# A sandwich of attention and feed-forward on one core: low halves on ScalarE's queue, products of block 1 ahead of the first scores, and a centred projection

## The chip, the cores and the metric

The kernel runs on one core of one Trainium2 chip. The metric is the device time of one execution in microseconds (us). The engines are named as the profile names them: PE (TensorE, matrix products), PEld (its weight loads), DVE (VectorE), ACT (ScalarE), POOL (GpSimd) and SP (SyncE, which only issues transfers here). ACT and POOL can issue transfers too; a transfer issue stands in the engine's own instruction order, so whatever the issue waits for, the instructions behind it wait for as well.

## What is computed

x is 4096 x 256, float32. With `ln` for a layer norm without weights:

```
x = x + ln(attention(ln(x)))          # 16 heads of 16, causal, out @ w_proj + b_proj
x = x + ln(ffn(ln(x)))                # 256 -> 1024 (gated) -> 1024 -> 1024 -> 256, ternary weights with scales
```

The part that the change touches is the inner `ln` behind the attention's projection: for each token, y = out @ w_proj + b_proj, then (y - mean(y)) / sqrt(var(y) + 1e-5), where mean and variance run over the 256 outputs of that token.

## The kernel before, in words

**Blocks.** The 4096 tokens are cut into eight blocks j = 0..7 of 512 (`QB`), each block into four tiles of 128 (`NT`). The 16 heads are cut into four groups g = 0..3. The attention walks through 32 items (j, g) in order. An item has 4j + 3 steps (`steps`, L876); a step makes one or two units of scores, 128 keys for 512 queries in two heads side by side, so a unit is 128 x 1024. The item (j, g) has 8j + 5 units, and the whole attention has 1056.

**A unit** goes through three engines. PE makes the scores into one of three PSUM buffers (`ps_s`, L843), DVE takes their maximum (L852), ACT takes their exponential into a tile `e` (L859). The maxima are not used by the same block's exponentials: they give the shift of the next block (`next_shift`, L1026) and a check at the end. Only block 0 takes its shift from its own first two units (L1171). On the diagonal POOL then clears what lies above it (L866). Later PE multiplies `e` with the values (L930) into one PSUM bank, which ACT copies out when the item is done (L953), and SP stores it.

**Queries and keys** are needed as a high half and a low half of each number (hi, lo). `features` (L519) makes them for half of the heads: two products into a bank (L525, `pk` or `pq`), an ACT pass that adds the bias (L534, tile `full`), a rounding to `hi` (L542) and the difference `lo` (L544). For blocks 0 and 1 DVE makes both halves, for the others POOL. Each half is then stored to DRAM twice (L549), in transfers of 8 heads x 16 x 512, and loaded again as rows of a head pair (L557). The tiles `full`, `hi` and `lo` exist once for keys and once for queries, so a second set waits for the stores of the first. The queue of a store is chosen at L548: for blocks 0 and 1 the low halves go by POOL's queue, all others by SP's.

**Background work.** `prep(j)` (L599) loads a block, normalises it, transposes it (L633), makes keys and queries for both halves of the heads, then the values (L650). `project(j)` (L273) gathers the finished attention of block j, multiplies by the weights `wp` (L314), adds the bias `bp`, makes the layer norm and stores `x1[j]`. Both are generators: every `yield` says what kind of piece comes next (PE, ACT or any). `Background.even` (L95), called after a step, gives at most one PE piece and one ACT piece for every 1 to 3 steps, depending on the block; `step` (L63) runs the next piece of the oldest job, and `finish` (L112) runs all that is left of a named job. `prep(j+2)` is added in item (j, 1), `project(j)` when the last item of block j has ended. In item (j, 3) the keys and queries of block j + 1 are forced if they are not there yet (L1137). `halve_weights` (L981) is a third job: four POOL passes (L1009 to L1012) on a piece of a feed-forward weight, one piece for every four steps.

**The layer norm in `project`** takes, for each of the four tiles of a block but the last one, one ACT pass for the mean (`mean_of`, L199, accumulating at L203), one ACT pass for the squared distances from it (`spread_of`, L207, at L211), then on POOL 1/sqrt (L215), shift and scale (L223) and the addition of x (L351). Each ACT pass is a piece of its own.

**The start** (L1102 to L1132) is written out by hand: the statistics of blocks 0 and 1, then `biases` (L1102), which folds the values' bias through `wp` into `bp` by one product (`pb`, L1106), then `prep(0)` up to the queries of the first half of the heads, the loads for the first two items, the rest of `prep(0)`, and then the walk over the items. `prep(1)` has only been normalised by then; its products run as pieces during block 0.

**Semaphores of transfers.** In the built program the transfers that SP and ACT issue take eight semaphores in turn, and one that takes a semaphore again first waits until the transfer that had it before has landed. POOL's transfers have eight others.

After the attention come the feed-forward layers, which start when the last block has ended; nothing in them is changed.

Of the kernel before, what the change touches and what calls it, by code (L numbers as in the profile page):

```python
# [10 lines left out]
F32 = mybir.dt.float32  # L11
F32R = mybir.dt.float32r
AF = mybir.ActivationFunctionType
ALU = mybir.AluOpType
AX = mybir.AxisListType
# [102 lines left out]
def sandwich_kernel(  # L118
# [80 lines left out]
    def mean_of(src, mv, t):  # L199

        lent.append(True)
        junk = const.tile([P, D], F32, tag="junk", name="junk")
        nc.scalar.activation(  # L203
            junk, src, AF.Identity, scale=-1.0 / D, accum_out=mv[:, t, 0:1]
        )

    def spread_of(src, mv, t):  # L207

        lent.append(True)
        junk = const.tile([P, D], F32, tag="junk", name="junk")  # L210
        nc.scalar.activation(  # L211
            junk, src, AF.Square, bias=mv[:, t, 0:1], accum_out=mv[:, t, 1:2]
        )

    def rstd_of(mv):  # L215
# [57 lines left out]
    def project(j, room):  # L273

        last = j == NB - 1
        xj = room.block(j)
        nc.sync.dma_start(out=xj, in_=rows(x, j))

        sums = stat.tile([P, H * QB // P], F32, tag="sums", name=f"sums_{j}")
        heads = weighed[j].rearrange("g (h e) n -> (g h) e n", e=HW)
        nc.sync.dma_start(out=sums, in_=heads[:, HD, :].rearrange("h (a n) -> h a n", a=8))
        for _ in range(5 if 1 < j < NB - 1 else 3):
            yield True
        if not last:
            nc.vector.tensor_reduce(least[:, j : j + 1], sums, AX.X, ALU.min)
        nc.vector.tensor_scalar(sums, sums, 1.0e-30, None, ALU.max)
        nc.vector.reciprocal(sums, sums)
        yield Background.HEAD  # L290
        nc.sync.dma_start(out=inverse[j].rearrange("h (a n) -> (h a) n", a=8), in_=sums)
        oT, inv = room.features(j)
        for c in range(DC):
            mine = slice(8 * c, 8 * (c + 1))
            nc.sync.dma_start(out=oT[:, c, :], in_=heads[mine, 0:HD, :])
            nc.sync.dma_start(
                out=inv[:, c, :],
                in_=inverse[j][mine, None, :].to_broadcast([8, HD, QB]),
            )
        for _ in range(4):  # L300
            yield True
        for c in range(DC):
            nc.gpsimd.tensor_tensor(oT[:, c, :], oT[:, c, :], inv[:, c, :], ALU.mult)
            yield True
        yield True
        yield Background.PE
        y = room.tokens(j)
        mv = stat.tile([P, NT, 2], F32, tag="mv", name=f"mvy_{j}")
        for half in range(0, NT, 2):
            ps = room.bank(f"py_{j}_{half}").rearrange("p (t f) -> p t f", t=2)  # L310
            for t in range(2):
                yield room.within(t)
                for c in range(DC):
                    nc.tensor.matmul(  # L314
                        ps[:, t, :],
                        lhsT=oT[:, c, (half + t) * P : (half + t + 1) * P],
                        rhs=wp[:, c, :],
                        start=(c == 0),
                        stop=(c == DC - 1),
                    )  # L320
            if last:
                nc.vector.tensor_tensor(
                    y[:, half : half + 2, :],
                    ps,
                    bp[:, None, :].to_broadcast([P, 2, D]),
                    ALU.add,
                )
                for t in range(half, half + 2):
                    layernorm_stats(y[:, t, :], mv, t)
            else:  # L330
                lent.append(True)
                nc.scalar.copy(y[:, half : half + 2, :], ps)
                nc.gpsimd.tensor_tensor(
                    y[:, half : half + 2, :],
                    y[:, half : half + 2, :],
                    bp[:, None, :].to_broadcast([P, 2, D]),
                    ALU.add,
                )
            yield Background.PE if half < NT - 2 else Background.ACT
        if not last:  # L340
            for t in range(NT):
                mean_of(y[:, t, :], mv, t)
                yield Background.ACT
                spread_of(y[:, t, :], mv, t)
                yield Background.ACT if t < NT - 1 else True
        rstd = (layernorm_rstd if last else rstd_of)(mv)
        for t in range(NT):
            (normalize if last else shift_and_scale)(
                y[:, t, :], y[:, t, :], mv, rstd, t, nc.gpsimd
            )  # L350
            nc.gpsimd.tensor_tensor(y[:, t, :], y[:, t, :], xj[:, t, :], ALU.add)  # L351
            yield True
        nc.sync.dma_start(out=rows(x1[j], 0), in_=y)
        yield True
# [49 lines left out]
    def attention(shared):  # L404
# [8 lines left out]
        with ExitStack() as actx:  # L413
# [19 lines left out]
            def two_banks(name):  # L433
                return ps_s.tile([P, 2, QB], F32, tag="s", name=name)
# [84 lines left out]
            def features(j, s, c, engine):  # L519
# [25 lines left out]
                for half, part in enumerate((hi, lo)):  # L545
                    for d in range(2):
                        at = (d, half) if i else (half, d)
                        queue = nc.gpsimd if shared and j < 2 and half else nc.sync  # L548
                        queue.dma_start(  # L549
                            out=halves_of[s, j][8 * c : 8 * (c + 1), at[0], at[1]], in_=part  # L550
                        )
# [549 lines left out]

            def biases():  # L1102
                nc.vector.tensor_scalar(bqk[:, 0:DC], bqk[:, 0:DC], SCALE, None, ALU.mult)
                ps = two_banks("pb")[:, 0, 0:D]
                for c in range(DC):
                    nc.tensor.matmul(  # L1106
                        ps,
                        lhsT=bv[:, c : c + 1].to_broadcast([P, P]),
                        rhs=wp[:, c, :],
                        start=(c == 0),  # L1110
                        stop=(c == DC - 1),
                    )
                nc.vector.tensor_tensor(bp, bp, ps, ALU.add)

            works = [prep(0, nc.vector), prep(1, nc.gpsimd)]
            for work in works:
# [10 lines left out]
            if shared:  # L1127
                bg.add(("prep", 1), works[1], PREP)
                bg.work[0][3] = Background.PE
            else:  # L1130
                while bg.piece(works[1]) is not False:
                    pass  # L1132
            mxs = {}
            for n, (j, g) in enumerate(items) if shared else ():
# [14 lines left out]
                if (j, g) == (NB - 1, G - 2):  # L1149
                    for _ in halving:  # L1150
                        pass
                    bg.add(("norm", 0), norm_block(0, room, first_features), NORM)
                if (j, g) == (NB - 1, G - 1):
                    W["h1"] = weight_pieces("h1", TAGS["h1"])
# [353 lines left out]
```

## Time and profile before

| what | value |
|---|---|
| median of 3 runs | 2053.86 us (2051.06 to 2056.44) |
| the profiled execution: its own time | 2048.42 us |
| span of the profiled execution, first to last instruction | 2046.5 us |
| first maximum of block 0 | 39.81 us |
| first maximum of block 1 | 92.84 us |
| last maximum of the attention ends | 1374.5 us |
| PE busy over the span | 1825.3 us (89%) |
| DVE busy over the span | 1609.8 us (79%) |
| ACT busy over the span | 1399.2 us (68%) |
| mean granted PE clock | 0.986 |

How to read what follows. A line of the timeline gives the start, the duration, the engine, the line in the kernel, the operation and its tiles; "x4" says that four such instructions are merged, and in brackets stands how long the engine sat idle before and who ended that. A line of the stage windows gives, for a stretch of the span, its length and then for each engine its busy time and its number of instructions, the granted clock of PE, the mean busy share of the 16 DMA engines and the bytes moved. "SPq" and "ACTq" are transfer issues, which don't count as busy time.

### The profile page before, as it was taken

Reading aid. Unit: us, or ns where it says so; the run is one execution under the profiler, and the core shown is the slowest. Engines: PE = TensorE matmul, PEld = TensorE weight load, DVE = VectorE, ACT = ScalarE, POOL = GpSimd, SP = SyncE. Lnnn points to the kernel's source line nnn. Section 1 sums busy time; section 2 is a strip of 40 time slices with the busy share of each in tenths; the row PEclk is TensorE's granted clock in tenths of the full one; section 3 lists DMA queues with packets and bytes.
Section 4 is the critical chain, followed back from the end, with each engine's and each line's share of the span. In section 5 each row is a group of like instructions: output and inputs, shape, how many; then the busy total and the mean of one; then the engine's idle time right before and its main releaser. Section 6 shows DMA issues by size and latency. Waiting matters only on the chain.

```text
span 2046.5 us, 28401 instructions
## 1 busy us (share of the span) xinstructions
PE 1825.3 (89%) x10518; PEld 932.5 (46%) x10518; DVE 1609.8 (79%) x1894; ACT 1399.2 (68%) x1598; POOL 552.2 (27%) x871
## 2 busy tenths in 40 slices
PE   4799989988888888888888887889999999999997
PEld 2333332322322322223222222228888888888886
DVE  3689998998999999999999999985546456465453
ACT  2699999999999999999999998982212222222221
POOL 3264545434435335333333110000120000000000
PEclk8899999999999999999999998999999999999999
DMA  6756645444235333553234213103100000000000
GB/s 168 229 179 219 191 133 180 147 154 159 98 131 183 116 103 124 161 163 115 76 136 156 98 44 101 63 9 114 53 11 21 15 7 21 1 21 21 1 11 15
DMA packets 134909, 202.09 MB, mean 99 GB/s; under 512 B 16064, under 2 KB 60736, under 8 KB 134752
## 3 DMA queue, kind: packets, MB, share of 16 engines
q1 hardware_dynamic: 130496, 194.56, 29.3%
q0 software_dynamic: 2480, 4.35, 1.0%
q8 instruction: 87, 1.43, 0.3%
q10 hardware_dynamic: 1776, 1.18, 0.3%
q14 instruction: 70, 0.57, 0.1%
HBM read 137.91 MB, written 62.13 MB: 98 GB/s over the span
## 4 chain that ended last, share of the span: by engine, by line
PE 46%; ACT 21%; DVE 19%; issue 6%; DMA 4%; POOL 2%; SPq 1%; ACTq 0%; POOLq 0%; DVEq 0%
PE z L1358 21%; ACT e_s L859 19%; DVE mx L852 18%; PE av L930 7%; PE s L843 7%; PE za L1358 3%; PE zb L1358 2%; PE pyf L1440 2%; DMA k<-k 1%; PE py L314 1%; PE pk L525 1%; PE pv L650 1%; PE pq L525 1%; ACT junk L211 1%; DMA q<-hiq 0%
## 5 line engine op out<-in xcount | busy, mean ns | idle before, releaser
L852 DVE TENSOR_REDUCE mx<-s 128x1 f32<-128x1024 f32 x1056 | 1219.8, 1217 | 72.1 <-PE s L843 66.6
L859 ACT ACTIVATE e_s<-s,shift 128x1024 f32<-128x1024 f32 x1056 | 1153.6, 1117 | 104.9 <-DVE mx L852 81.9
L843 PE MATMUL s<-q,k 64*128 64x512 f32 (+3 forms) x2304 | 517.7, 468 | 161.2 <-ACT e_s L859 144.7
L930 PE MATMUL av<-e_s,v 128*32 128x512 f32 (+2 forms) x4576 | 572.8, 575 | 7.9 <-POOL e_s L866 5.7
L843 PEld LDWEIGHTS s<-q,k 64*128 64x128 f32 x2304 | 208.9, 185 | 752.9 <-ACT e_s L859 652.2
L1425 ACT ACTIVATE fb<-z,sh 128x512 f32<-128x512 f32 x128 | 88.1, 689 | 364.8 <-PE z L1358 340.2
L1358 PE MATMUL z<-hb_0l,h 128*128 128x512 f32 x512 | 199.5, 390 | 0.0
L1358 PE MATMUL z<-hb_0h,h 128*128 128x512 f32 x512 | 199.5, 390 | 0.0
L866 POOL TENSOR_SCALAR_AFFINE_SELECT e_s<-e_s 128x256 f32<-128x256 f32 (+1 forms) x224 | 94.7, 440 | 337.4 <-ACT e_s L859 337.4
L233 POOL TENSOR_TENSOR rstd<-ve,neghalf 128x4 f32<-128x4 f32 (+1 forms) x22 | 20.8, 944 | 608.8 <-DVE ve L231 603.0
L930 PEld LDWEIGHTS av<-e_s,v 128*32 128x32 f32 x4576 | 97.2, 109 | 151.5 <-issue 116.1
L1325 DVE CAST hb_1h<-fb 128x512 fp32r<-128x512 f32 x64 | 27.4, 428 | 155.7 <-ACT fb L1425 155.7
L1402 ACT ACTIVATE sl<-za,s 128x512 f32<-128x512 f32 x64 | 44.0, 690 | 120.4 <-PE za L1358 60.9
L1325 DVE CAST hb_0h<-fb 128x512 fp32r<-128x512 f32 x64 | 28.1, 440 | 99.6 <-ACT fb L1425 99.6
L1358 PEld LDWEIGHTS z<-hb_0h,h 128*128 128x128 f32 x512 | 96.1, 188 | 20.0
L1358 PEld LDWEIGHTS z<-hb_0l,h 128*128 128x128 f32 x512 | 96.2, 188 | 19.8
L1011 POOL TENSOR_SCALAR wc<-wc 128x256 f32<-128x256 f32 x88 | 75.8, 861 | 7.8
L1010 POOL TENSOR_TENSOR wc<-wc,wh 128x256 f32<-128x256 f32 x88 | 64.3, 730 | 7.2
L1012 POOL TENSOR_TENSOR fit<-fit,wc 128x256 f32<-128x256 f32 x88 | 64.2, 730 | 7.3
L1009 POOL CAST wh<-wc 128x256 fp32r<-128x256 f32 x88 | 35.0, 397 | 108.4 <-DMA wc<-in_h_t_dram 75.9
L1440 PE MATMUL pyf<-w,hb_1l 128*128 128x256 f32 x256 | 61.8, 284 | 0.0
L1440 PE MATMUL pyf<-w,hb_1h 128*128 128x256 f32 x256 | 61.7, 283 | 0.0
(257 smaller groups left out, 1970.3 us busy)
## 6 DMA issues: line engine op xcount, KB each, us to landing
k<-k SPq DMA_DIRECT2D x288, 256.0 KB
q<-q SPq DMA_DIRECT2D x64, 256.0 KB
x<-in_x_dram SPq DMA_DIRECT2D x16, 512.0 KB
k<-hik SPq DMA_DIRECT2D x32, 256.0 KB
q<-hiq SPq DMA_DIRECT2D x32, 256.0 KB
wc<-in_h_t_dram SPq DMA_DIRECT2D x64, 128.0 KB
r_h<-wh SPq DMA_DIRECT2D x64, 128.0 KB
h<-r_h SPq DMA_DIRECT2D x32, 256.0 KB
```

Of the source, the lines that this page charges most:

```text
L843: nc.tensor.matmul(self.both[:, i, col : col + n], lhsT=kT[G * j + g, c, pr][r, tt * P : (tt + 1) * P], rhs=qT[j, g][pr][r, QB - n :], sta ...
L852: nc.vector.tensor_reduce(next(columns), self.both.rearrange("p a n -> p (a n)"), AX.X, ALU.max)
L859: nc.scalar.activation(e, self.both, AF.Exp, bias=shifts[j])
L866: nc.gpsimd.affine_select(out=here, in_=here, compare_op=ALU.is_ge, fill=0.0, base=0, pattern=[[0, here.shape[1]], [1, P]], channel_multip ...
L930: nc.tensor.matmul(self.av[h * HW : (h + 1) * HW, QB - n :], lhsT=vb[kt // NT][:, kt % NT, o : o + HW], rhs=of(es, h), start=(kt == 0 or k ...
L1010: nc.gpsimd.tensor_tensor(w, w, hi, ALU.subtract)
L1011: nc.gpsimd.tensor_scalar(w, w, 0.0, None, ALU.is_equal)
L1012: nc.gpsimd.tensor_tensor(fit, fit, w, ALU.mult)
L1325: nc.vector.tensor_copy(hi, full)
L1358: nc.tensor.matmul(ps, lhsT=w[c], rhs=single(part[:, c, :]), start=(c == 0 and i == 0), stop=(c == kc - 1 and i == parts - 1),)
L1425: nc.scalar.activation(h, z, AF.Gelu, scale=sc[:, oc : oc + 1])
L1440: nc.tensor.matmul(ps[:, 0:D], lhsT=single(part[:, c, t * P : (t + 1) * P]), rhs=(w3_r if halves else w3_sb)[:, c, :], start=(c == 0 and i ...
```

## The change

It has four parts.

1. The queue of the low halves (L548): for block 0 they are issued by ACT instead of POOL; block 1 stays on POOL, the others on SP.
2. Before the walk over the items, `prep(1)` is stepped until the keys of its first half of the heads are stored: two groups of four transposes and the two products of one `pk`, with the copies, rounding and stores that belong to them. These then stand ahead of the first scores in the order of PE, ACT and DVE.
3. In `biases` the projection weights are centred in place: each row of `wp` (one input, 256 outputs) loses its mean over the outputs, before the product `pb` reads it; after `pb` is added, `bp` loses its own mean. Then every y has mean zero, and for all blocks but the last, `project` leaves the mean pass out, takes the squares about 0.0 and scales without a shift.
4. Ahead of the item (7, 2), `project(6)` is finished by force before the norm of block 0 is added.

```diff
-    def spread_of(src, mv, t):
+    def spread_of(src, mv, t, shift=None):
...
-            junk, src, AF.Square, bias=mv[:, t, 0:1], accum_out=mv[:, t, 1:2]
+            junk,
+            src,
+            AF.Square,
+            bias=mv[:, t, 0:1] if shift is None else shift,
+            accum_out=mv[:, t, 1:2],
         )
...
             for t in range(NT):
-                mean_of(y[:, t, :], mv, t)
-                yield Background.ACT
-                spread_of(y[:, t, :], mv, t)
+                spread_of(y[:, t, :], mv, t, 0.0)
                 yield Background.ACT if t < NT - 1 else True
         rstd = (layernorm_rstd if last else rstd_of)(mv)
         for t in range(NT):
-            (normalize if last else shift_and_scale)(
-                y[:, t, :], y[:, t, :], mv, rstd, t, nc.gpsimd
-            )
+            if last:
+                normalize(y[:, t, :], y[:, t, :], mv, rstd, t, nc.gpsimd)
+            else:
+                nc.gpsimd.tensor_scalar(
+                    y[:, t, :], y[:, t, :], rstd[:, t : t + 1], None, ALU.mult
+                )
...
-                        queue = nc.gpsimd if shared and j < 2 and half else nc.sync
+                        queue = (nc.scalar, nc.gpsimd)[j] if shared and j < 2 and half else nc.sync
...
             def biases():
                 nc.vector.tensor_scalar(bqk[:, 0:DC], bqk[:, 0:DC], SCALE, None, ALU.mult)
+                mean = stat.tile([P, DC], F32, tag="mean", name="mean")
+                nc.vector.tensor_reduce(mean, wp, AX.X, ALU.add)
+                nc.vector.tensor_scalar(mean, mean, -1.0 / D, None, ALU.mult)
+                for c in range(DC):
+                    nc.vector.tensor_scalar(
+                        wp[:, c, :], wp[:, c, :], mean[:, c : c + 1], None, ALU.add
+                    )
                 ps = two_banks("pb")[:, 0, 0:D]
...
                 nc.vector.tensor_tensor(bp, bp, ps, ALU.add)
+                nc.vector.tensor_reduce(mean[:, 0:1], bp, AX.X, ALU.add)
+                nc.vector.tensor_scalar(mean[:, 0:1], mean[:, 0:1], -1.0 / D, None, ALU.mult)
+                nc.vector.tensor_scalar(bp, bp, mean[:, 0:1], None, ALU.add)
...
                 bg.add(("prep", 1), works[1], PREP)
                 bg.work[0][3] = Background.PE
+                while ("k", 1, 0) not in stored:
+                    bg.step()
...
                 if (j, g) == (NB - 1, G - 2):
                     for _ in halving:
                         pass
+                    bg.finish(("project", NB - 2))
                     bg.add(("norm", 0), norm_block(0, room, first_features), NORM)
```

## The prediction, made before the changed kernel ran

> **What bounds the kernel now.** I read first the page's busy times and groups, then the stage windows (a stretch for each block, from its first maximum to the next block's), then the timeline where a stretch loses time.
>
> ```profile
> PE 1825.3 (89%) x10518; PEld 932.5 (46%) x10518; DVE 1609.8 (79%) x1894; ACT 1399.2 (68%) x1598; POOL 552.2 (27%) x871
> L852 DVE TENSOR_REDUCE mx<-s 128x1 f32<-128x1024 f32 x1056 | 1219.8, 1217 | 72.1 <-PE s L843 66.6
> L859 ACT ACTIVATE e_s<-s,shift 128x1024 f32<-128x1024 f32 x1056 | 1153.6, 1117 | 104.9 <-DVE mx L852 81.9
> ```
>
> PE leads over the whole span, but that mixes two stages. Up to 1374.5 us every unit costs DVE 1.22 and ACT 1.12 us.
>
> ```profile
> 39.81:92.84 53.03, 39.91 (x212) 17.32 (x212) 29.00 (x34) 30.02 (x41) 16.95 (x38) 0.77 0.72 222
> 92.84:167.92 75.08, 68.06 (x444) 25.71 (x444) 63.50 (x60) 66.84 (x88) 37.40 (x64) 1.00 0.62 204
> 274.94:422.75 147.81, 135.39 (x844) 45.27 (x842) 137.62 (x124) 136.80 (x170) 68.39 (x108) 0.99 0.46 147
> 825.19:1078.98 253.79, 218.67 (x1402) 68.27 (x1402) 246.15 (x222) 240.85 (x243) 95.01 (x146) 1.00 0.41 131
> 1078.98:1374.50 295.52, 245.06 (x1562) 72.38 (x1562) 288.17 (x276) 275.48 (x270) 37.95 (x63) 0.98 0.24 80
> ```
>
> The third and fourth busy times are DVE and ACT. In blocks 1 to 7 both run nearly full, ACT ahead only in blocks 1 and 2; block 0 (first row) leaves DVE idle for 24 of 53 us. So there are two places to gain in: block 0, and the few stalls of DVE later. The feed-forward stage after 1374.5 isn't touched.
>
> **Part 3, the mean passes.** They are 4 a block in 7 blocks:
>
> ```profile
> L203 ACT ACTIVATE junk<-y x28: 406/407/510, 171.4 to 1197.6; 128x256 f32<-128x256 f32 x28
> ```
>
> With the read-out of the sum that follows, ACT is held 0.51 us (one starts at 76.08, the read-out ends at 76.59). 28 x 0.51 = 14.3 us is the upper bound, if ACT set the pace at every one. The rows say that it mostly doesn't: item (7,1), 1152.23 to 1222.65, holds four of them and four spread passes and takes 70.42 / 61 units = 1.154 us a unit, while (7,0) with none takes 73.25 / 61 = 1.201, and (6,1) with none 64.61 / 53 = 1.219 against (6,2) with three, 63.59 / 53 = 1.200. In (7,1) DVE has a backlog (57 maxima in 65.39 us without a gap), which is the cover. Only block 2, where ACT is the fuller engine, should pay for its four: 2 us at most. I take **-1**, bounds 0 and -14.3.
>
> **Part 3, what it does to POOL's order.** Four pieces fewer, one for every 2 or 3 steps of 2.5 us, let the y work on POOL (1/sqrt, four scalings of 0.55, four additions of 0.73, some 6.4 us) start 20 to 30 us earlier. That matters at the ends of items, where POOL must clear the diagonal. Timeline of POOL at the end of (3,1):
>
> ```profile
> 340.49 0.61 POOL L542 CAST hik<-fullk 128x512 fp32r<-128x512 f32 x1
> 341.19 1.27 POOL L544 TENSOR_TENSOR lok<-fullk,hik 128x512 fp32r<-128x512 f32 x1
> 342.44 0.55 POOL L224 TENSOR_SCALAR y<-y,mvy,rstd 128x256 f32<-128x256 f32 x1
> 343.08 0.73 POOL L351 TENSOR_TENSOR y<-y,x 128x256 f32<-128x256 f32 x1
> ...
> 346.68 2.79 POOL L866 TENSOR_SCALAR_AFFINE_SELECT e_s<-e_s 128x256 f32<-128x256 f32 x7
> ```
>
> and what DVE sees:
>
> ```profile
> 350.20 2.35 DVE L852 TENSOR_REDUCE mx<-s 128x1 f32<-128x1024 f32 x2 [3.23 <-PE s L843]
> ```
>
> Seven clearings run back to back, so all were waiting behind the queue; PE waits for the first (1.82 us at 347.15), the next scores stand behind it, and DVE idles 3.23 us. Two more such stalls: 3.08 us at 471.78 (y work at 467.33 just ahead of the clearings) and 1.57 at 274.94 (the bp addition at 269.06, 1/sqrt and a scaling ahead). The built program's new order has no y work at those three ends. At the first, rounding can start when its input is there (337.83 instead of 340.49) and the pair y of 1.3 us is gone: 2.7 + 1.3 exceeds the stall; what stays is rounding, lo and a weight piece (4.8 us) just ahead, the pattern that costs 0.77 at 608.48. So -2.4. At the second only the pair (1.28) goes: -1.3. At the third -1.3. But two ends, of (2,1) and (2,2), now get the pattern of 608.48: +0.6 each. Sum: **-4**; bounds -7.9 (all three stalls) and +2.3 (none gone, three new ones of 0.77).
>
> **Parts 1, 2 and the centring: the start.** The path before, in the timeline:
>
> ```profile
> 23.24 2.60 SPq L549 DMA_DIRECT2D q<-hiq  x2
> 33.79 0.84 SPq L557 DMA_DIRECT2D q<-q  x2
> ...
> 41.72 1.23 DVE L852 TENSOR_REDUCE mx<-s 128x1 f32<-128x1024 f32 x1 [0.69 <-PE s L843]
> ```
>
> Stores, loads, first maxima. The new steps in order:
> - *Centring.* The reduction of 512 numbers costs 0.68 (like `least` at 1156.76), the scaling 0.15, a subtraction of 256 0.35 (four normalisations of x in 1.38). DVE is free at 13.23, so `pb` starts at about 14.6 instead of 12.37, and PE's transposes stand behind it: +2.25 for all that follows. The second half (1.3 us on bp) lies in DVE's idle 5.14 us ahead of the first rounding: free.
> - *Low stores.* ACT must wait for `lo` (1.2 us after `full`) and issue two transfers. ACT as issuer of stores isn't in the trace; its loads at the start take 0.42 to 0.60, SP's stores 0.59, POOL's 0.60: I take 0.6. The next `full` slips by 0.4. Keys and queries of the first half are 2 MB of stores; before, they landed by 33.6. While only SP's stores ran, DMA was half busy:
>
> ```profile
> 45.00:48.00 3.00, 2.31 (x12) 1.55 (x12) 2.33 (x2) 3.00 (x4) 0.82 (x2) 0.50 0.52 201
> ```
>
>  If ACT's stores share that half, 2.1 MB at 201 GB/s from 24.2 on end at 34.6; if they use the other, last issue 27.8 plus some 5 us, 32.8. I take 34, so the first loads go out where they did. The Trainium skill (DMA: Bandwidth & Descriptors, "Why a DMA increments its semaphore by 16 and not by 1") says that a transfer issued by SP or ACT with 8 rows outside takes the lowest-numbered 8 of 16 engines, while POOL's rotate; this speaks against part 1 and would give 34.6; the half-busy row agrees with the 8.
> - *ACT stuck.* For the second half of the heads ACT waits for each `lo`, whose tile waits for the earlier store to land (29.2 and 34): its last low store goes out at about 36. Behind it stand both copies of v (before 30.46 and 33.13), then the copies of the new products. PE follows: values 36.7 to 38.7, transposes to 41.8, `pk` 42.6 to 44.7. DVE's rounding for block 1 stands ahead of the first maximum and also waits for the second high store of block 0 (44.5). First maximum 46.7, second until 49, instead of 39.81 and 42.95: **+6.3**. Bounds: +4.4 (ACT's issues free), +9 (PE at half clock, as the 0.77 of the first window tells of part of it, doubles the 2 us of `pk`).
> - *Block 0 itself.* Two waits for loads go: DVE idles 4.7 us up to 80.28 and 3.95 up to 92.84, because block 1's stores leave late (queries' second half at 78.4 to 80.6). With four products done, those stand four steps earlier, at about 70, and no product is forced in item (0,3). Going through the order row by row I get first maxima of the items at 58, 70, 80 and 89 (before 53.54, 65.12, 80.28, 92.84). From 46.7 to 80 it regains 6.5 (49.2 to 80 against 42.95 to 80.28); the last item takes 9 instead of 12.56.
>
>  Sum: 6.3 - 6.5 - 3.6 = -3.8, so **-4**; bounds: -8.6 (late by 3 only, waits gone, 3 us of forced pieces gone) and +9 (late, nothing regained).
>
> **Part 4** forces nothing: in the new order project(6) ends in item (7,1), as its store at 1212.0 does already. 0; if it weren't done, its 6.4 us of POOL would be late there.
>
> **Sum:** -4 - 4 - 1 = -9 us, against the profiled execution 2048.42 - 9 = 2039.4. The median shown is 5.4 higher, so against it 2053.86 - 9 = **2045**.
>
> **Rivals.**
> - *A: ACT is the pace.* If all 28 passes count in full: 8 + 14.3, so 2031.5. For it: ACT is ahead in blocks 1 and 2. Against: (7,1) above.
> - *B: nothing left.* POOL's work is the same and only moves: new ends lose what old ones gain, and the start comes out even: 2052. For it: rounding and weight pieces still stand ahead of the ends of (2,1), (2,2), (3,1).
> - *C: slower.* ACT's queue behind the low stores decides the start: first maximum after about 52 us, SP's loads for (0,3) and (1,0) behind the later stores as before, block 1 from 100 on: +7, with the stalls' gain eaten: 2061. It decides once block 1 starts after 97. For it: three engines in order behind one landing. Against: block 0 has 8.65 us of waits to give.
>
> **How the numbers follow.** Forecast 0.50, A 0.10, B 0.27, C 0.13. A measurement of this kernel can tell about 0.3% (6.2 us) from no change. The forecast's own range is 2039 to 2051; of its 0.50, 0.08 lie within 0.3%. Faster 0.42 + 0.10 = 0.52; same 0.08 + 0.27 = 0.35; slower 0.13. The range takes in B and half of the way to A and C: 2035 to 2056.
>
> **What would show it.** Right: the first maximum at 45 to 49, block 1's at 87 to 91, DVE's gaps at the starts of (3,0), (3,2), (4,1) under 2 us each, the time a unit in (7,1) unchanged. Wrong: block 1 starting at 93 or later; new gaps over 2 us at (2,2) or (2,3); items of blocks 5 and 6 that get shorter by half a us for each pass taken out.

## The result

The changed kernel takes 2056.93 us (median of 20 runs, 2052.17 to 2064.64), the kernel before, timed beside it, 2051.99 (20 runs): ratio 1.0024, 95% interval 1.0015 to 1.0034. It is 4.9 us slower, where 9 us faster was forecast. Rival C (slower, 2061) named the two marks that it decides from, first maximum after 52 and block 1 after 97, and both were passed. Of the mechanism it named one half: ACT's queue, where the runs below show two chains.

The page of the changed kernel's profile (span 2053.5 us, own time 2055.23), the rows that answer to those of before:

```profile
PE 1828.0 (89%) x10518; PEld 935.1 (46%) x10518; DVE 1609.7 (78%) x1901; ACT 1395.6 (68%) x1542; POOL 559.0 (27%) x863
L857 DVE TENSOR_REDUCE mx<-s 128x1 f32<-128x1024 f32 x1056 | 1217.4, 1216 | 67.5 <-PE s L848 64.2
L864 ACT ACTIVATE e_s<-s,shift 128x1024 f32<-128x1024 f32 x1056 | 1160.0, 1117 | 94.3 <-DVE mx L857 72.9
```

The long rows hardly move: the time isn't in the work of a unit. Stage windows for blocks 0, 1, 3, 6 and 7, as for the kernel before, cut at the changed kernel's own first maxima (the last number of such a row is GB/s, the one before it the busy share of the DMA engines):

```profile
54.25:102.64 48.39, 34.05 (x198) 15.04 (x198) 27.59 (x32) 26.08 (x31) 15.45 (x33) 0.82 0.66 195
102.64:178.60 75.96, 68.12 (x440) 25.03 (x440) 63.38 (x61) 69.75 (x95) 39.01 (x70) 1.00 0.64 206
287.51:435.68 148.17, 136.81 (x848) 46.63 (x848) 137.30 (x125) 137.79 (x165) 71.13 (x109) 0.98 0.47 150
837.40:1089.21 251.81, 215.91 (x1390) 66.87 (x1390) 245.72 (x221) 239.76 (x232) 94.92 (x144) 1.00 0.41 132
1089.21:1382.98 293.77, 244.59 (x1560) 72.83 (x1562) 287.44 (x275) 275.34 (x261) 39.40 (x63) 0.98 0.24 80
```

Read the first number after each stretch, its length. Block 0 from its first maximum is shorter (48.39 against 53.03), but begins 14.4 us later (54.25 against 39.81), so block 1 begins 9.8 later (102.64 against 92.84). Blocks 6 and 7 are 1.98 and 1.75 shorter. Block 3, where the stall of 3.23 us at (3,2) is indeed gone, isn't. Blocks 1 to 7 together take 1280.3 against 1281.6.

**The start**, in the changed kernel's timeline:

```profile
39.63 1.20 ACTq L554 DMA_DIRECT2D q<-loq  x2
...
43.55 0.58 ACT L663 COPY v<-pv 128x512 f32<-128x512 f32 x1 [2.08 <-PE pv L655]
...
45.16 2.53 SPq L554 DMA_DIRECT2D k<-hik  x2
...
46.87 3.27 PE L530 MATMUL pk<-xT,wqk 128*128 128x512 f32 x4 [0.67 <-ACT xT L642]
...
50.07 1.07 PE L848 MATMUL s<-q,k 64*128 64x512 f32 x4
50.23 0.69 ACT L539 ACTIVATE fullk<-pk,bqk 128x512 f32<-128x512 f32 x1 [3.42 <-PE pk L530]
53.18 0.43 DVE L547 CAST hik<-fullk 128x512 fp32r<-128x512 f32 x1 [13.57 <-DMA k<-hik]
...
54.25 2.35 DVE L857 TENSOR_REDUCE mx<-s 128x1 f32<-128x1024 f32 x2
```

Two chains meet in the rounding `hik` of block 1, behind which the first maximum stands. One is ACT's: last low store at 39.63, the copies of v behind it (the second at 43.55; before at 33.13), then block 1's transposes, `pk` at about half clock (3.27 us; the granted clock reads 0.59 from 46.8 to 50.2), `fullk` ready at 50.92. The other is the tile `hi`: it is free only when the second high half of block 0's keys, issued by SP at 45.16 behind the loads, has landed, at 53.18. The scores of the first units have been there since 51.1. The chain that ended last, followed back, shows what held the second one up:

```profile
34.05 6.07 DMA k<-lok
...
40.18 6.91 DMA k<-k
...
47.11 5.94 DMA k<-hik
...
53.18 0.44 DVE hik L547
```

A low store of ACT lands, then a load that SP issued behind it, then the high store behind the load. So in this profile ACT's low stores stand at the head of both chains.

**The new stalls** that took the place of those at (3,0) and (3,2), here in item (2,1), which takes 29.50 us instead of 26.10:

```profile
216.74 1.55 SPq L164 DMA_DIRECT2D x<-in_x_dram  x1
...
225.59 0.42 ACT L203 ACTIVATE junk<-x 128x256 f32<-128x256 f32 x1 [2.54 <-DMA x<-in_x_dram]
...
227.69 2.40 DVE L857 TENSOR_REDUCE mx<-s 128x1 f32<-128x1024 f32 x2 [2.34 <-PE s L848]
```

ACT reaches `prep`'s first pass over x before x has landed, and stands still with the exponentials behind it; DVE follows 2 us later. These first passes wait for x three times, 4.14 us in block 0, 2.54 in (2,1) and 1.58 in (3,1); before once, 0.70 in block 0.

### The profile page after: what moved, and what is told of

Read it like the earlier page. It is cut to its first block, busy times and chain, and to the rows that moved or that the text cites. A ratio compares the mean times of both kernels' runs of the same rounds, so it can differ in the third digit from the quotient of the medians.

```text
span 2053.5 us, 28396 instructions
## 1 busy us (share of the span) xinstructions
PE 1828.0 (89%) x10518; PEld 935.1 (46%) x10518; DVE 1609.7 (78%) x1901; ACT 1395.6 (68%) x1542; POOL 559.0 (27%) x863
## 3 DMA queue, kind: packets, MB, share of 16 engines
q0 software_dynamic: 1328, 2.25, 0.5%
## 4 chain that ended last, share of the span: by engine, by line
PE 47%; DVE 23%; ACT 18%; DMA 4%; issue 3%; POOL 2%; SPq 1%; ACTq 0%; POOLq 0%; DVEq 0%
PE z L1376 22%; DVE mx L857 22%; ACT e_s L864 16%; PE av L935 6%; PE s L848 6%; PE za L1376 3%; PE zb L1376 3%; PE pyf L1458 3%; PE py L318 1%; PE pv L655 1%; DMA k<-k 1%; DMA x<-in_x_dram 1%; PE pk L530 1%; PE pq L530 1%; DMA k<-lok 1%
```

## The experiments

Ratios are to the kernel before, timed beside each. Positions come from one profiled execution each, in us; "1 to 3" and "4 to 7" are the lengths of those blocks. "Shared" and "own" say whether block 1's first halves use the common tiles. Every kernel with centring also has part 4.

| kernel | low halves | products first | centring | ratio (95%) | first max. | block 1 | 1 to 3 | 4 to 7 |
|---|---|---|---|---|---|---|---|---|
| before | POOL | no | none | 1 | 39.81 | 92.84 | 329.9 | 951.7 |
| e9, before again | POOL | no | none | - | 44.05 | 95.50 | 332.3 | 952.5 |
| changed | ACT | shared | early | 1.0024 (1.0015 to 1.0034) | 54.25 | 102.64 | 333.0 | 947.3 |
| e1 | ACT | no | none | 1.0010 (0.9999 to 1.0021) | 45.01 | 97.09 | 331.4 | 952.5 |
| e2 | POOL | shared | none | 1.0006 (0.9997 to 1.0016) | 49.50 | 97.36 | 328.0 | 951.0 |
| e3 | POOL | no | early | 0.9990 (0.9979 to 1.0000) | 46.04 | 97.36 | 329.0 | 945.9 |
| e4 | ACT | shared | late | 1.0011 (1.0001 to 1.0021) | 52.06 | 100.78 | 331.0 | 946.5 |
| e5 | POOL | no | late | 0.9962 (0.9949 to 0.9975) | 43.55 | 94.14 | 328.2 | 948.2 |
| e6 | POOL | own | none | 0.9976 (0.9965 to 0.9987) | 45.91 | 92.64 | 328.2 | 951.0 |
| e7 | POOL | behind 2 units | none | 1.0017 (1.0008 to 1.0026) | 44.15 | 102.21 | 329.0 | 951.4 |
| e8 | POOL | no | late, spread twice | 1.0027 (1.0017 to 1.0037) | 44.65 | 95.36 | 333.6 | 955.0 |
| e10 | POOL | own | late | 0.9963 (0.9952 to 0.9975) | 45.81 | 94.42 | 332.6 | 945.7 |
| e11 | POOL | shared | early | 1.0017 (1.0003 to 1.0030) | 54.82 | 101.79 | 333.4 | 946.8 |
| e12 | ACT | own | early | 1.0021 (1.0007 to 1.0034) | 53.30 | 102.67 | 329.9 | 947.2 |
| e13 | POOL | shared | late | 1.0009 (0.9996 to 1.0021) | 48.15 | 95.83 | 334.5 | 945.4 |
| e14 | POOL | own | early | 0.9980 (0.9968 to 0.9992) | 46.88 | 96.09 | 328.5 | 945.7 |
| e15 | as e10, first pass six steps after the load | | | 1.0014 (1.0004 to 1.0025) | 43.95 | 93.16 | 327.9 | 956.2 |
| e16 | as e15, two operands | | | 0.9998 (0.9987 to 1.0009) | 45.33 | 93.29 | 328.8 | 956.1 |
| e17 | as e10, first pass two steps later in two blocks | | | 0.9945 (0.9931 to 0.9958) | 44.45 | 93.63 | 328.4 | 946.9 |
| e18 | ACT | no | early | 0.9987 (0.9978 to 0.9997) | 45.77 | 98.84 | 328.6 | 946.4 |

### One part at a time

**e1**, part 1 alone (the line of the queue only).

> The kernel before with part 1 alone: block 0's low halves issued by ACT. Theory (the start is late because ACT's order holds its copies behind low stores, and because the four products then stand ahead of the first scores): this part alone gives the smaller share. ACT's last low store at about 36 instead of nothing, the two copies of v behind it (30.46 and 33.13 before, 38 and 41 now), SP's loads of queries at 38 to 39 instead of 33.79; first maximum 44 to 46 instead of 39.81, block 1 at 93 to 95 instead of 92.84, since block 0 has waits of 8.65 us to give. Time 0 to +3 us against before. Rival 1 (the four products alone make the loss): first maximum within 1 us of 39.81 and time within 1 us of before. Rival 2 (ACT's order makes all of it): first maximum after 50, block 1 after 99, time +6 or more.

**e2**, part 2 alone.

```diff
                 bg.work[0][3] = Background.PE
+                while ("k", 1, 0) not in stored:
+                    bg.step()
```

> The kernel before with part 2 alone: four transposes in two groups, one pair of products, their copies, rounding and stores ahead of the first scores; low halves stay with POOL, nothing centred. Theory: first maximum later by the two transposes (some 3 us), the product at half clock (3.3) and DVE's rounding that waits for the store of the second high half of block 0's keys (landed 45 or later): 47 to 50 instead of 39.81, block 1 at 96 to 99 instead of 92.84; time +3 to +6 us. Rival 1 (the products make the whole loss): block 1 at 101 to 103, time +8 to +10. Rival 2 (ACT's order makes it): first maximum by 44, block 1 at 88 to 92, time 0 to -5 us, that is this part alone would gain.

**e3**, part 3 as in the change, with the forced end of project(6).

> The kernel before with part 3 (and the forced end of project(6), which moves nothing): weights centred ahead of pb, no mean pass. Theory: first maximum +2.2 (centring ahead of pb and of the transposes), about 42; block 1 at 93 to 95; blocks 1 to 7 shorter by about 1 us (new stalls at (2,1) and (3,1) from the load of x take back what the ends of (3,0), (3,2) give). Time -1 to +2 us against before. Rival 1 (the late steady state is the loss, the mean passes covered something): blocks 1 to 7 longer, time +3 or more. Rival 2 (ACT is the pace and the mean passes count): blocks 1 to 7 shorter by over 5 us, time -4 or better.

The first maximum came at 45.01, 49.50 and 46.04, the time at +0.10, +0.06 and -0.10%. No part alone is the loss. The sum of the three, 0.06%, is a quarter of the 0.24% of the changed kernel; each ratio is known to about 0.1%, so this only suggests that the parts act on each other. e1 and e2 kept to their theories at the first maximum, but e2's time was +1 us, where +3 to +6 was expected. e3 fits rival 2 in part: its blocks 4 to 7 are 6 us shorter.

**e9**, the kernel before once more.

> The kernel before, unchanged, profiled once more. In the first profile the first product pk took 1.99 us (17.28 to 19.3) and the first maximum came at 39.81; in the runs with products only, low halves only, and products behind the first units, whose orders are the same up to there, pk took 3.78 and first maxima came 2 us later at least. Theory (the half clock at the start is drawn anew in each execution, and the first profile of before drew well): pk 3.5 to 3.8, first maximum at 42 to 45, block 1 at 95 to 98, so that 2 to 4 us of the +9.8 between the two profiles' block 1 are the clock's. Rival (before is early by its order): pk 2.0, first maximum within 1 us of 39.81, block 1 within 1 us of 92.84.

```profile
17.68 3.78 PE L525 MATMUL pk<-xT,wqk 128*128 128x512 f32 x4 [0.68 <-ACT xT L637]
...
44.05 2.35 DVE L852 TENSOR_REDUCE mx<-s 128x1 f32<-128x1024 f32 x2 [6.83 <-PE s L843]
```

The theory held: the same program, `pk` 3.78 instead of 1.99 and the first maximum 4.2 later. Of all the profiles here, only the first of before and e13 have that `pk` at the full pace. That this is the clock is inferred: the granted clock reads 1.00 over both first `pk`, so the profile doesn't show it there. Where it does show it, the factor is the same: a `pv` of the changed kernel took 3.67 instead of 2.00 us at a granted clock of 0.55 (37.1 to 40.9). The product itself is 1.8 of the 4.2; the rest came with the landings behind it.

So the prediction counted from a lucky start; against the usual one the changed kernel is late by 10.2 at the first maximum and by 7.1 at block 1. Its blocks 1 to 7 then take 4.4 less (1280.3 against 1284.7), so that the attention ends 2.8 later; against the first profile it ends 8.5 later. The 4.9 of the medians lies between. Differences of positions below some 4 us at the start and 3 at block 1 say nothing by themselves.

### The changed kernel with one part taken out

**e18**, without the products.

> The changed kernel without the four products ahead of the first scores; ACT's low stores and early centring stay. Theory (ACT's order and the products together make the late start, each delays what the other waits for): first maximum at 46 to 48 instead of 54.25, block 1 at 97 to 99 instead of 102.64, blocks 1 to 7 as with centring alone, 1275 to 1278; time -5 to -7 against the changed kernel, 2050 to 2052. Rival (as with the other single parts, taking this one alone shows the next wait): block 1 at 101 or later, time within 3 us of the changed kernel.

**e11**, the low halves with POOL.

> The changed kernel with block 0's low halves issued by POOL as before; products ahead and early centring stay. Theory (ACT's order holds the copies of v and of block 1's transposes behind the low stores: in the changed kernel the second copy of v came at 43.55, with the products alone at 35.27): first maximum 50 to 52 instead of 54.25, bound then by DVE's rounding that waits for the high half's store; block 1 at 99 to 101; time -2 to -4 against the changed kernel. Rival 1 (DVE's wait for the landing is the last one anyway and ACT's delay is hidden under it): first maximum within 1 us of 54.25, time within 1 us. Rival 2 (ACT's order is most of the loss): first maximum by 48, time -5 or better.

**e12**, own tiles for block 1's first halves (the tiles of a key that is loaded only in block 2).

```diff
-                hi = piece(f"hi{i}", f"hi{s}_{j}_{c}")
+                own = (s, j, c) == ("k", 1, 0)
+                hi = piece("k15_0" if own else f"hi{i}", f"hi{s}_{j}_{c}")
...
-                lo = piece(f"lo{i}", f"lo{s}_{j}_{c}")
+                lo = piece("k15_1" if own else f"lo{i}", f"lo{s}_{j}_{c}")
```

> The changed kernel with tiles of their own for the halves of block 1's first keys; all else stays, ACT's low stores and early centring too. In the changed kernel the scores stood ready at 50.9, the rounding waited until 53.18, the first maximum came at 54.25. Theory (with ACT's low stores the products come so late that the rounding waits little): first maximum at 51 to 53, time -1 to -3 against the changed kernel, less than the -6 to -7 that the same edit gave with the products alone. Rival (the waiting rounding is the main cost here too): first maximum by 49, time -4 or better.

**e4**, the centring behind `pb`.

```diff
-                mean = stat.tile([P, DC], F32, tag="mean", name="mean")
-                nc.vector.tensor_reduce(mean, wp, AX.X, ALU.add)
...
                 ps = two_banks("pb")[:, 0, 0:D]
...
                 nc.vector.tensor_tensor(bp, bp, ps, ALU.add)
+                mean = stat.tile([P, DC], F32, tag="mean", name="mean")
+                nc.vector.tensor_reduce(mean, wp, AX.X, ALU.add)
...
```

> The changed kernel, with the centring of the weights moved behind the product pb (and behind the addition to bp, whose own mean is taken off anyway); nothing else. Theory: pb at 12.4 instead of 14.58, and what stands behind it earlier by the same, so first maximum 52 instead of 54.25 and block 1 at 100.5 instead of 102.64; time -2 us against the changed kernel (about +3 against before). Rival 1 (the landings of the stores, not PE's order, set the first maximum): first maximum within 0.7 us of 54.25 and time within 1 us of the changed kernel. Rival 2 (the centring was a third or more of the +9.8 of the start): first maximum by 50, time -3.5 or better.

Of these four, only the one without the products has an early first maximum (45.77), and its time falls by 0.37%, to just below that of before. e4 came as its theory had it (52.06, 100.78, 0.13% less). e11 went the way of its rival 1 at the first maximum (its time fell by 0.07%), and e12 gave less than its theory: each takes one chain away, and the first maximum stays (54.82, 53.30). The timelines tell why. e11, ACT free:

```profile
45.21 0.69 ACT L539 ACTIVATE fullk<-pk,bqk 128x512 f32<-128x512 f32 x1 [2.12 <-PE pk L530]
...
48.50 0.50 PE L848 MATMUL s<-q,k 64*128 64x512 f32 x2 [0.39 <-DMA k<-k]
...
53.75 0.43 DVE L547 CAST hik<-fullk 128x512 fp32r<-128x512 f32 x1 [12.42 <-DMA k<-hik]
```

`fullk` is there 5 us sooner than in the changed kernel, but the rounding still waits for the landing. Without ACT's stores, SP's loads wait for a high store of the queries instead and go out at 40.21. Up to 1.8 us of the 54.82 are luck: here the first `pq` took 3.78 too, where the changed kernel has 1.98. e12, the tile free:

```profile
47.80 3.62 PE L530 MATMUL pk<-xT,wqk 128*128 128x512 f32 x4 [0.68 <-ACT xT L643]
...
52.23 0.43 DVE L548 CAST hik<-fullk 128x512 fp32r<-128x512 f32 x1 [11.70 <-ACT fullk L539]
```

The wait is now named `ACT fullk`: the other chain.

### Two parts mended

**e14**, low halves with POOL and own tiles.

> The changed kernel with low halves with POOL and tiles of their own for block 1's first halves; the centring stays ahead of pb. Theory (early centring costs its 2.2 us on the path to the first maximum and nothing more): first maximum at 46.5 to 48.5, 2 to 2.5 later than with late centring (45.81), time 2 to 3 us over that run, 2046 to 2048. Rival (early centring moves all behind it into a worse stretch of the clock or of the queues, and costs 4 or more): time 2049 or more.

**e13**, low halves with POOL and late centring, shared tiles.

> The changed kernel with two of its parts mended: low halves of block 0 with POOL, and centring behind pb; the products ahead keep the shared tiles. Alone, the first gave about -1.5 and the second about -3 us against the changed kernel; both and the tiles of their own gave about -12. Theory (ACT's order, the early centring and DVE's waiting rounding are three waits side by side that end within 3 us of each other, so taking one shows the next): first maximum at 48 to 51, block 1 at 96 to 98, time -7 to -9 against the changed kernel, that is 2048 to 2050. Rival (the effects just add): time -4 to -5, 2052 to 2053.

e14 shows the two chains side by side. With early centring and the products ahead, the first maximum comes at 54.25 (ACT, shared), 54.82 (POOL, shared), 53.30 (ACT, own), and at 46.88 only when both waits are gone; the ratio goes from 1.0024, 1.0017 and 1.0021 to 0.9980. Its timeline:

```profile
45.81 0.43 DVE L548 CAST hik<-fullk 128x512 fp32r<-128x512 f32 x1 [5.78 <-ACT fullk L539]
...
46.88 2.35 DVE L858 TENSOR_REDUCE mx<-s 128x1 f32<-128x1024 f32 x2
```

e13 drew the fast `pk`, so its 48.15 can't be set beside the others. Its time, 1.0009, is its rival's: with the tile still shared, mending the two other parts just adds their small gains.

### What the products and the mean passes are worth

**e6**, part 2 alone with own tiles (e2 and the edit of e12).

> Part 2 alone, as in the run with the products only, but the high and low halves of block 1's first keys get tiles of their own, so DVE's rounding doesn't wait until the second high half of block 0's keys has landed. In the run without this, scores stood ready at 43.5 and the first maximum came at 49.50, behind a rounding that waited until 48.43. Theory (that wait is the greater part of what the products cost): first maximum at 43.5 to 45.5, block 1 at 91 to 93.5 instead of 97.36, time -3 to -5 against the run with the products only, -2 to -4 against before. Rival 1 (the cost is PE's and ACT's order ahead of the scores): first maximum at 48 or later, time as there. Rival 2 (what is gained at the first maximum is lost again because the loads for items (0,2) and (0,3) come no earlier): first maximum at 44, block 1 still at 96 to 98.

The time confirms it: 0.9976 against 1.0006 with shared tiles. The products gain when nothing waits behind their rounding; the first maximum, 45.91, is a little later than the theory had it, with bad luck at the start: its first three groups of products all took 3.7 to 3.8 us.

**e7**, the same products forced behind the first two units.

```diff
                         for unit in units:
                             unit.finish()
+                        while ("k", 1, 0) not in stored:
+                            bg.step()
```

> The kernel before with the four products of part 2 forced behind the first two units (their maxima, the shift and their exponentials) instead of ahead of the first scores. Theory (the products gain some 5 us inside block 0, which took 47.9 us with them against 53.0, and cost only by their place): first maximum at 39 to 41, the next ones 3 to 5 us later than before, block 1 at 88 to 91 instead of 92.84, time -2 to -5 against before. Rival (they cost the same anywhere in block 0, since PE, ACT and DVE are in order behind them): block 1 at 92 or later, time 0 or more.

The rival won, and by more than it said: item (0,0) takes 22.11 us instead of 12.36 to 13.74, block 1 begins at 102.21. Forced in one go behind the maxima, the products hold up the remaining scores of (0,0); ahead of the first scores they lie in time in which PE waits for loads.

**e5**, part 3 with late centring.

> The kernel before with part 3 alone, the weights centred behind the product pb instead of ahead of it; low halves with POOL, no products ahead. Theory (early centring costs 2.2 us at the start plus what follows it, the missing mean passes gain 4 to 6 us from block 1 on): first maximum 39 to 41, block 1 at 92 to 94, blocks 1 to 7 at 1275 to 1277 us instead of 1281.6; time -4 to -6 against before, and so the first version that beats both. Rival 1 (the 1275.0 of the run with early centring was luck of the order on POOL, not ACT's time): blocks 1 to 7 at 1279 to 1282, time within 2 us of before. Rival 2 (the late start there was the clock's luck, not the centring): same start as there, first maximum 45 or later.

2043.82 against 2051.08: 0.9962, better than expected. e3 and e5 differ in the place of the centring alone; early costs 0.28% by the ratios, some 3 us by the positions of block 1. The two other pairs give less: 0.13% (the changed kernel and e4) and 0.17% (e14 and e10, below).

**e8**, e5 with every spread pass taken twice in its piece.

```diff
                 spread_of(y[:, t, :], mv, t, 0.0)
+                spread_of(y[:, t, :], mv, t, 0.0)
```

> The run with late centring alone, with each spread pass of y taken twice in the same piece: ACT's work is that of before (28 passes and read-outs of 0.51 us more), the number of pieces and so POOL's order are those without the mean pass. Theory (what part 3 gains from block 1 on is ACT's time): blocks 1 to 7 4 to 6 us longer than with late centring alone, near 1281, time within 2 us of before. Rival (it is the order of the pieces on POOL): blocks 1 to 7 within 1.5 us of late centring alone, time -4 or better against before.

2058.15 - 2043.82 = 14.3 us for 28 passes: the theory's direction at three times its size, 0.51 each, the whole of ACT's time. A pass that makes a piece longer is paid in full here. As a piece of its own it is paid in part: over blocks 4 to 7 the six profiles with the mean pass (before twice, e1, e2, e6, e7) take 951.0 to 952.5, the eleven without it (the changed kernel, e3 to e5, e10 to e14, e17, e18) 945.4 to 948.2. By their means (951.7 and 946.5) that is 5.1 us for 16 passes, 0.32 each.

### Why the gains don't add

**e10**, e5 and e6 together.

> Late centring without the mean pass, and the four products ahead of the first scores with tiles of their own for the halves of block 1's first keys; low halves of block 0 with POOL as before. Theory (the two gains, -7.3 from block 1 on and -4.6 at the start, lie in different stages and add): first maximum at 44 to 46, block 1 at 91 to 94, blocks 1 to 7 at 1273 to 1278, time -9 to -12 against before. Rival 1 (the x loads come too late for the earlier pieces, as in the changed kernel, where (2,1) took 29.50 instead of 25.5): (2,1) 28 or more, blocks 1 to 7 at 1279 or more, time -6 to -8. Rival 2 (they overlap): time no better than -7.3.

0.9963, no better than e5, as rivals 1 and 2 had it, though (2,1) and blocks 1 to 7 (27.65 and 1278.3) stay just under rival 1's marks. From block 1 on, its first passes wait 4.6 us for x (e5: 1.9, e6: 1.4), and (3,1) takes 40.75 us.

**e15**, e10 with the first pass over x six steps after the load.

```diff
-                for _ in range(2):
+                for _ in range(2 if j < 2 else 6):
                     yield True
                 yield Background.ACT
```

> The best of both (late centring, no mean pass, products ahead with tiles of their own, low halves with POOL), and the first pass over a block's x given six steps after its load instead of two, for blocks 2 to 7. In the run without this, that pass waited for the load 8.4 us in three places, and DVE stood still 1.85 us in item (2,1) and 5.2 us in (3,1). Theory (these waits are why the two gains didn't add): no wait for x above 1 us, (2,1) at 25.5 to 26.5 instead of 27.65, (3,1) at 36 to 38 instead of 40.75, blocks 1 to 7 at 1272 to 1275 instead of 1278.3, time -3 to -5 against that run, 2039 to 2042. Rival (the same time is lost elsewhere, since the pieces move into other places of POOL's order): blocks 1 to 7 within 1.5 us of 1278, time within 1.5 of 2044.5.

No wait for x is left, (3,1) takes 35.73. But the work put off was forced at the ends of blocks:

```profile
149.41 1.99 PE L530 MATMUL pq<-xT,wqk 128*128 128x512 f32 x4 [0.84 <-ACT fullk L539]
...
151.87 1.22 DVE L858 TENSOR_REDUCE mx<-s 128x1 f32<-128x1024 f32 x1 [5.71 <-PE s L849]
```

DVE stands still for 5.71 us behind forced products at the end of (1,2), and (5,0) takes 63.40 instead of 55.29. The rival was right, and more: 1.0014.

**e16**, e15 with y scaled by two operands (a column of zeros is added first).

> The same as the run with x in time, with y scaled on POOL by two operands (add of a column of zeros, then the product) as before, instead of one: 0.55 us each before against 0.93 now, x 28 = 10.5 us of POOL's 559. Theory (POOL has time off the path; only the ends of items see it): scalings at 0.55 us, time within 1.5 us of the run with x in time. Rival (POOL's order at the ends of items decides, so 1.5 us less for each block counts): blocks 1 to 7 shorter by 2 us or more.

The scalings are back at 0.55 us, and blocks 1 to 7 take 1284.9 against 1284.1, so in the two profiles POOL's time isn't on the path. But the median of e16 is 3.6 us lower (2050.70 against 2054.30), outside the theory's 1.5, and the two profiled executions (2053.07 and 2051.35) stand the other way round. So it stays open whether the scalings cost time.

**e17**, e10 with two steps more for blocks 4 and 5 alone.

```diff
-                for _ in range(2):
+                for _ in range(4 if j in (4, 5) else 2):
```

> Late centring without the mean pass, products ahead with tiles of their own, low halves with POOL, and the first pass over x two steps later for blocks 4 and 5 alone (those whose load came late in items (2,1) and (3,1)); all other blocks as before. With six steps after the load for all of blocks 2 to 7 the stalls of (2,1) and (3,1) went (26.08 and 35.73 instead of 27.65 and 40.75), but (1,2) took 25.54 instead of 20.56 and (5,0) 63.40 instead of 55.29, since work put off was forced there. Theory (late x loads are why the gains didn't add): (2,1) at 26 to 26.6, (3,1) at 35.5 to 37.5, no item longer by over 2 us in return; blocks 1 to 7 at 1273 to 1275, time -3 to -5 against the 2045 of the same kernel without it, some 2041. Rival (any later start costs as much elsewhere): blocks 1 to 7 at 1277 or more, time within 1.5 us of 2045.

2040.6 us, 0.9945 (0.9931 to 0.9958, from 5 runs): the theory's time, and a kernel faster than both. (3,1) takes 37.68, passes wait for x only once, 3.1 us in block 0, and no item pays for it. This agrees with late loads as the reason, but doesn't show it alone: the interval touches that of e10 (0.9952 to 0.9975), and e14, which has the order of e10 from block 1 on and no later pass, drew 36.76 in (3,1) and 1274.2 for blocks 1 to 7 (e17: 1275.3). Among the profiles with that order and x not put off, (3,1) is long where the pass waits long: 36.63 to 36.86 with waits of 1.2 to 1.4 us, 38.55 with 1.58, 38.93 to 40.75 with 2.4 to 2.5.

## Why the prediction was wrong, step by step

- **ACT stuck (+6.3) is the step that failed.** "First maximum 46.7" had both chains in it, yet let each end too early. It put `pk` at 42.6 to 44.7; it came at 46.87 and took 3.27, since ACT's last low store went out at 39.63 (said: about 36), `pv` ran at about half clock (3.67 us, granted clock 0.55) and the first `pk` took 3.73. It put the landing at 44.5, on the assumption that "the first loads go out where they did" (33.79). They went out at 38.85, since the stores that they read landed only then; SP issued the second high store behind them from 45.16 on, and it landed at 53.18. So the wait for the landing was the term that was sized too small, and the upper bound of +9 came from ACT's chain alone: measured are +14.4 against the first profile and +10.2 against e9. e11, e12 and e14 show that the chains cover each other, so no estimate of one of them could have found the cost.
- **Block 0 itself (-6.5 - 3.6).** Forecast 42.3 us from the first maximum to block 1, measured 48.39. The gain is real but smaller, 4.6 and 3.1 us against the two profiles of before (53.03 and 51.45), where 10.1 was counted. The products have it when the start is free (e6: 46.73).
- **Centring (+2.25).** Measured 2.2 at `pb` (14.58 against 12.37), and 2.2 at the first maximum (e4; 2.5 by e3 and e5, 1.1 by e14 and e10). Right; that it must stand ahead of `pb` was taken over from the change and not questioned.
- **Low stores.** Landed by 38.8, not by 34. That ACT's stores share a half of DMA with SP's fits. While the stores run, the changed kernel's DMA is half busy, and before, with POOL's stores, it isn't (second last column):

```profile
26.00:38.00 12.00, 5.28 (x12) 2.11 (x11) 2.24 (x4) 2.06 (x3) 0.00 (x0) 0.97 0.51 174
```

```profile
24.00:33.00 9.00, 6.67 (x22) 3.56 (x20) 1.12 (x2) 1.96 (x3) 2.37 (x4) 1.00 0.80 210
```

 e1, with this part alone, has 0.52 (24 to 38 us); e2, with POOL's stores, 0.80 (26 to 35). So the rule that the prediction cited against part 1 from the Trainium skill (DMA: Bandwidth & Descriptors, "Why a DMA increments its semaphore by 16 and not by 1") agrees with these rows, and its 34.6 was still too early.
- **Mean passes (-1)**, mis-sized: 0.32 us a pass in blocks 4 to 7. The step generalised from (7,1), the item with the best cover; there the four passes give 0.64 (70.42 to 69.78), but in (6,2) three give 1.6, half a us each, one of the prediction's own signs of being wrong. e5 has both terms of part 3 without the early centring, forecast at -5: 7.3 us by the medians.
- **POOL's order (-4).** The stalls named went (3.23 and 1.57) or shrank (3.08 to 1.78): -6.1. What stood next was left out: pieces that come earlier meet a load of x that doesn't. In (2,1) and (3,1) DVE's stalls around that wait are 2.34 + 1.37 and 1.38 + 1.24 + 0.65 = 7.0 us.
- **Part 4 (0).** Nothing to see of it; not tried alone.

Shown: the start is late because the products stand ahead of the first scores (e18), and there two waits cover each other (e14). Shown too: the two gains, missing passes and earlier products, are real (e5, e6). That they add once x is in time agrees with e17 (0.55% of the 0.62% of their sum), but rests on 5 runs and one profile. Only argued: that the 0.32 us of a pass is ACT's time and not the order of pieces; e8 prices a longer piece, not a missing one.

## What to carry to other kernels

When two engines wait behind one another at the head of a kernel, follow every chain into the instruction that stands last, and price each as if the others were gone; taking one away tells little while another ends within a few us of it. A rounding or copy into a shared tile waits for the landing of what was stored from it (in e11 its input was ready at 45.90 and it began at 53.75), and an in-order engine hands that wait to all behind it: give moved work tiles of its own. And when pieces come earlier, look up the load that feeds the next job.

## What was not expected of the hardware

- The pace of PE at the start is drawn anew: the same first `pk` took 1.98 to 1.99 us in 2 of 20 profiles and 3.4 to 3.8 in the others, and between two profiles of one program the first maximum moved by 4.2. That it is the clock is inferred (see e9). The Trainium skill (TensorE: Matmul & The Clock Gate, "Part 1: The HAM clock gate") says that the window over which activity is judged runs freely and doesn't start with the kernel; two profiles of one program that differ agree with that.
- POOL's scaling of 128x256 takes longer with one operand (926 ns) than with two (554 ns); the changed kernel's row, then that of e16:

```profile
L353 POOL TENSOR_SCALAR y<-y,rstd 128x256 f32<-128x256 f32 x28 | 25.9, 926 | 0.7
```

```profile
L355 POOL TENSOR_SCALAR y<-y,zero,rstd 128x256 f32<-128x256 f32 x28 | 15.5, 554 | 0.8
```
